# Four transformer-like layers on one core: loads in order of need, an extra step in three attentions' weaves, cross attention's keys and values inside the norm

## The chip, the cores and the metric

One core of one Trainium2 chip. The metric is the device time of one execution, in microseconds (us). Durations and waits below come from one profiled execution; a profile counts from its first instruction.

## What is computed

Input x has 2048 tokens (32 sequences of 64) of 256 channels, fp32, and a context of the same size. Four layers run one after the other on x:

- Layer 0: a transformer block, y = ln1(x), self attention with 16 heads of 16 channels, cross attention to the context (16 x 16), and an MLP to 1024 channels and back, with additive and multiplicative masks:

```python
scores = einsum('bhqd,bhkd->bhqk', q, k) / sqrt(HD)
scores = scores * mask - 10000.0 * (1.0 - mask)
probs = softmax(scores)
```

- Layer 1: a recurrent block. A state of 8 x 8 for each of 32 heads runs over the 64 tokens of a sequence, `s = k v + w * s`, read out with r; a group norm, a gate, a projection, and a second half with squared relu.
- Layer 2: two cross attentions to the context with 16 heads of 128 channels and one learned key and value beside the 64, then an MLP.
- Layer 3: a cross attention with 16 heads of 16 channels under a key mask, then an MLP. Its result is the output.

## The kernel before, in words

**Groups and stages.** The tokens are cut in 4 groups g of 512 (8 sequences). A layer of a group is a Python generator that issues instructions and yields after each step. `weave(main, (light, rate), ...)` runs `main` step by step and advances each light generator by `rate` steps for every step of main; the rates stand in `FILL` and `RATES` at the file's end. The stages:

1. layer 0 of group 0 with a filler (0.6): about 20 to 221 us
2. layer 1 of group 0 with layer 0 of group 1 (1.25) and the filler (0.7): to 528
3. layer 2 of group 0 with layer 1 of group 1 and then layer 0 of group 2 (1.13): to 965
4. layer 2 of group 1 with layer 1 of group 2 and layer 0 of group 3 (1.13): to 1403
5. layer 2 of group 2 with layer 1 of group 3 and layer 3 of group 0 (0.93): to 1773
6. layer 2 of group 3 with layer 3 of groups 1 and 2 (0.46): to about 2100
7. layer 3 of group 3 with what is left of that (1.6)

The filler, `keep`, computes layer 2's first keys and values ahead. One unit of it is four matmuls (k2p_f twice, L165; v2p_f twice, L726), one ACT step (fk, L928), one DVE step (fv, L937) and two stores of 256 KB (kd, vd) to device memory. Within what the generators issue, a scheduler places instructions on each engine by readiness; each engine then works strictly in its own order.

**Names.** DVE is VectorE, ACT ScalarE, POOL GpSimd, PE TensorE, SP the engine that issues most transfers. In tile names the letter is the norm or attention: a is layer 0's self attention, b its cross attention, c its MLP; d and e are layer 1; f, o2 and h layer 2; i and j layer 3's attention and MLP. The number behind it is the group: b1 is group 1's cross attention in layer 0.

**`norm`** (L167 to 195): statistics (L174, L176), a power on POOL (L178), the normed x (xn, L180), a bias row added to x (L185), and PE transposes to channel-major (nt, L190) with scale and offset (y, L192 and L194).

**`attn16`** (L220 to 315): for each half c of the channels, queries qT (L227) and keys kb (L232, L233; two copies, masked to one of two heads each); values vp (L242), spread by ACT and DVE into block-diagonal vb (L254, L256), with a yield after each of those four. Then four steps (c, rp): `weights` makes 16 score matmuls (sp, L269) into a two-bank tile, of which there are two; the mask (DVE product and POOL sum in layer 0, L380/381 and L385/386; one DVE sum in layer 3, L668); the softmax (L200 to 209: DVE maximum, DVE subtraction, ACT exponential, DVE sum, DVE reciprocal); and the POOL product with the reciprocal (L276). `turned` transposes the weights (tp, L286) and copies them (pt, L287); `gathered` multiplies with vb (pv, L295) and adds the bias (oT, L299). Two steps of weights are made ahead:

```python
ahead = [weights(*steps[0])]
yield
ahead.append(weights(*steps[1]))
yield
```

**Layer 1's states** (L550 to 566): vj on PE, a product on DVE (L559), two scans on DVE (L565) and a product on POOL (L566), also made two ahead, then gathered with PE (op, L588).

**Layer 2's attention** `bias_attn`: two groups of four heads run at a time, in turn (`interleave`). After the second half's product with the values (pv, L817) and its scaling (o, L828) one yield stands before the output product (`add_linear`: al_o, L328, added to x at L341).

**Loads.** At the start SP issues constants, x0, two weight slots of 512 KB, x1 to x3; POOL's queue takes the context c0 to c3 (512 KB each); ACT's takes masks and the initial state. DVE prepares masks (L153 to 159, L375, L376) as soon as they are issued in program order.

Of the kernel before, what the change touches and what calls it, by code (L numbers as in the profile page):

```python
# [14 lines left out]
P = 128  # L15
# [53 lines left out]
def kernel(  # L69
# [25 lines left out]
    def bank(name):  # L95
        return psum1.tile([P, 512], F32, tag="b1", name=name)
# [40 lines left out]

    xs, cs = [], []
    for g in range(G):
        xg = xp.tile([P, TT, D], F32, name=f"x{g}")  # L140
        nc.sync.dma_start(xg, x_in[:, g])
        xs.append(xg)
        if g == 0:
            first = [slot(L0_AT), slot(L0_AT + 1)]
    for g in range(G):
        cg = xp.tile([P, NC, GT], F32, name=f"c{g}")
        nc.gpsimd.dma_start(cg, cT[:, g])
        cs.append(cg)
    ms = cp.tile([P, S], F32, name="ms")
    for h in range(2):  # L150
        nc.scalar.dma_start(ms[64 * h : 64 * h + 64, :], m_self)
    ns = cp.tile([P, S], F32, name="ns")
    V.tensor_scalar(ns, ms, 10000.0, -10000.0, ALU.mult, ALU.add)  # L153
    V.tensor_scalar_mul(ms, ms, 0.25)
# [3 lines left out]
    at3 = VAT["L3_xattn_q_b"]  # L158
    V.tensor_scalar_mul(bq3, vt[:, at3 : at3 + NC], 0.25)

# [5 lines left out]

    def norm(xg, wname, bname, nm, y, xn, then=None):  # L167

# [12 lines left out]
        if then is not None:  # L181
# [3 lines left out]
            PL.tensor_tensor(xg, xg, row.to_broadcast([P, TT, D]), ALU.add)  # L185
        yield
        for c in range(NC):
            tp = bank(f"nt_{nm}_{c}")
            for i in range(TT):
                PE.transpose(tp[:, i * P : (i + 1) * P], xn[:, i, c * P : (c + 1) * P], ident)  # L190
# [4 lines left out]
        return y  # L195

# [145 lines left out]

    def mlp(xg, y, w1, w2, b1, func, new, nm):
        hs = []
# [22 lines left out]
    def layer0(g, work):  # L367

        xg = xs[g]
        wa = first if g == 0 else [slot(L0_AT), slot(L0_AT + 1)]  # L370
        mc = sm.tile([P, 4, S], F32, tag="mc", name=f"mc{g}", bufs=1)
        for h in range(2):
            nc.scalar.dma_start(mc[64 * h : 64 * h + 64, :, :], m_cross[:, h, 4 * g : 4 * g + 4, :])
        nr = sm.tile([P, 4, S], F32, tag="nr", name=f"nr{g}", bufs=1)
        V.tensor_scalar(nr, mc, 10000.0, -10000.0, ALU.mult, ALU.add)  # L375
        V.tensor_scalar_mul(mc, mc, 0.25)  # L376

# [9 lines left out]

        def normed(i, nm, then):
            y = work.four(f"y_{nm}")
            return norm(xg, f"L0_xattn_ln{i}_s", f"L0_xattn_ln{i}_b", nm, y, work.four(f"xn_{nm}"), then)  # L390

        y = yield from normed(1, f"a{g}", "L0_xattn_b_ao")
        yield
        bn = "L0_xattn_b_qkv"
        o = yield from attn16(
            y, y, (wa[0], 0, 512), (wa[0], 256, 512), (wa[1], 0),
            cols(bn, 0), cols(bn, 2), cols(bn, 4), mask_self, work, f"a{g}",
        )
        add_linear(xg, wa[1], 512, halves(o), f"a{g}")
        yield  # L400
        wb = [slot(L0_AT + 2), slot(L0_AT + 3)]
        y = yield from normed(2, f"b{g}", "L0_xattn_b_co")
        yield
        bn = "L0_xattn_b_kv"
        o = yield from attn16(
            y, cs[g], (wb[0], 0, D), (wb[0], 512, D), (wb[1], 0),
            cols("L0_xattn_b_q"), cols(bn, 0), cols(bn, 2), mask_cross, work, f"b{g}",
        )
        add_linear(xg, wb[1], 512, halves(o), f"b{g}")
# [30 lines left out]
    def layer1(g, work):  # L440
# [213 lines left out]
    def layer3(g, work, wp=lw):  # L654
# [15 lines left out]
        y = yield from norm(  # L670
            xg, "L3_xattn_ln1_w", "L3_xattn_ln1_b", f"i{g}", work.four(f"y_i{g}"), work.four(f"xn_i{g}"),
            "L3_xattn_cproj_b",
        )
        yield
        o = yield from attn16(
            y, cs[g], (wa[0], 0, D), (wa[0], 512, D), (wa[1], 0),
            [bq3[:, c : c + 1] for c in range(NC)], cols("L3_xattn_k_b"), cols("L3_xattn_v_b"), mask_keys,
            work, f"i{g}", 0.25,
        )
        add_linear(xg, wa[1], 512, halves(o), f"i{g}")  # L680
# [7 lines left out]
        w2 = [slot(L3_AT + 4 + i, wp) for i in range(2)]  # L688
        yield from mlp(xg, y, w1, w2, "L3_xattn_fc_b", AF.Gelu_apprx_tanh, pairs(work, f"j{g}"), f"j{g}")
        nc.sync.dma_start(out[:, g], xg)  # L690

# [39 lines left out]
    def bias_attn(a, qd, g, hh, pool, w2, work):  # L731
# [128 lines left out]
        gathered(1, p1)  # L860
        yield
        add_linear(xs[g], wo, 0, outs, f"o2{nm}")
        yield
# [234 lines left out]
```

## Time and profile before

| | us |
|---|---|
| median of 3 runs | 2218.61 (2216.74 to 2219.75) |
| the profiled execution's own time | 2216.37 |
| its span, first to last instruction | 2214.6 |
| PE busy | 2057.4 (93%) |
| DVE, ACT, POOL busy | 1097.3, 632.9, 597.5 |

The profile's columns: an instruction group is named by line, engine and operation, then output<-input with tile names (buffer numbers left out), then its shape and count. PE is TensorE's matmuls, PEld its weight loads, which overlap them. A wait is named by the group that waited, an arrow, and the group whose end released it. PEclk is the TensorE clock that was granted: 1.00 is full. In the rows of 40 slices each digit is a tenth of busy share (or of full clock), one digit for 55.4 us.

### The profile page before, as it was taken

The numbers are of one execution on the slowest core, as the hardware profiler recorded it, in microseconds if no ns is written. First come the engines' busy times: TensorE is split into PE (matmuls) and PEld (weight loads), VectorE is DVE, ScalarE is ACT, GpSimd is POOL, SyncE is SP. The second block draws the span as 40 slices with busy tenths as digits, with TensorE's granted clock in tenths as the row PEclk, the third lists the DMA queues.
The fourth block names the chain that finished last, engine by engine and source line by source line (L and its number), as shares of the span: only waits on it lengthen the run. The fifth ranks groups of instructions, "written<-read, shape, count | busy, mean of one in ns | idle before, by whom it ended". The sixth has DMA issues, their size and how long they took to land. (4 is left out here: it accounts for less than half of the span.)

```text
span 2214.6 us, 36273 instructions
## 1 busy us (share of the span) xinstructions
PE 2057.4 (93%) x15264; PEld 1242.9 (56%) x15264; DVE 1097.3 (50%) x1885; ACT 632.9 (29%) x1000; POOL 597.5 (27%) x498
## 2 busy tenths in 40 slices
PE   5889998899999898999997999999999999999998
PEld 3445444354555465755554656555566767565665
DVE  3552557423655636335556463266564355424661
ACT  1222322132321322232313132322233233222442
POOL 2331344213423314214324141233221112200220
PEclk9999998999999999999998999999999999999999
DMA  7233231226412212243121123341213342213010
GB/s 247 93 106 118 93 110 57 93 101 229 141 49 64 66 41 63 92 132 109 55 62 58 42 79 96 121 134 44 86 45 108 100 152 69 78 51 94 22 41 20
DMA packets 79794, 197.25 MB, mean 89 GB/s; under 512 B 9616, under 2 KB 14352, under 8 KB 79632
## 3 DMA queue, kind: packets, MB, share of 16 engines
q1 hardware_dynamic: 77472, 191.88, 27.1%
q8 instruction: 121, 1.98, 0.4%
q0 software_dynamic: 576, 2.10, 0.3%
q10 hardware_dynamic: 1584, 0.95, 0.2%
q14 instruction: 41, 0.34, 0.1%
HBM read 158.98 MB, written 35.91 MB: 88 GB/s over the span
## 5 line engine op out<-in xcount | busy, mean ns | idle before, releaser
L165 PE MATMUL q2p<-h,w 128*128 128x512 f32 x512 | 245.4, 612 | 6.8 <-DMA w<-in_wts 3.2
L328 PE MATMUL al_o<-w,o 128*128 128x256 f32 x1024 | 235.1, 388 | 11.7 <-DVE o L828 10.7
L328 PEld LDWEIGHTS al_o<-w,o 128*128 128x128 f32 x1024 | 196.6, 194 | 52.6 <-issue 20.6
L778 ACT ACTIVATE q<-q2p,vt 128x512 f32<-128x512 f32 x128 | 87.5, 685 | 278.9 <-PE q2p L165 275.7
L165 PEld LDWEIGHTS q2p<-h,w 128*128 128x128 f32 x512 | 94.9, 193 | 123.6 <-issue 105.5
L796 POOL TENSOR_TENSOR pn<-s,sm 128x512 f32<-128x512 f32 x64 | 69.7, 1091 | 285.2 <-DVE sm L209 198.2
L165 PE MATMUL k2p_f<-c,w 128*128 128x512 f32 x256 | 131.2, 634 | 4.9 <-DMA w<-in_wts 2.8
L726 PE MATMUL v2p_f<-w,c 128*128 128x512 f32 x256 | 122.4, 601 | 0.0
L165 PE MATMUL k2p<-c,w 128*128 128x512 f32 x256 | 120.7, 597 | 0.0
L726 PE MATMUL v2p<-w,c 128*128 128x512 f32 x256 | 119.1, 609 | 1.1 <-DVE k L764 1.1
L566 POOL TENSOR_TENSOR a<-a,r 128x1024 f32<-128x1024 f32 x32 | 76.1, 2378 | 109.8 <-DVE a L565 96.4
L937 DVE TENSOR_TENSOR fv<-v2p_f,vb 128x512 f32<-128x512 f32 x64 | 43.9, 687 | 124.7 <-PE v2p_f L726 124.7
L928 ACT ACTIVATE fk<-k2p_f,vt 128x512 f32<-128x512 f32 x64 | 43.9, 686 | 175.4 <-PE k2p_f L165 146.8
L341 DVE TENSOR_TENSOR x<-al_o,x 128x512 f32<-128x512 f32 x64 | 43.6, 683 | 101.2 <-PE al_o L328 101.2
L828 DVE TENSOR_SCALAR o<-pv,vt 128x256 f32<-128x256 f32 x128 | 55.8, 473 | 76.6 <-PE pv L817 76.4
L764 DVE TENSOR_SCALAR k<-k2p,vt 128x512 f32<-128x512 f32 x64 | 47.4, 743 | 91.4 <-PE k2p L165 91.4
L788 PEld LDWEIGHTS s2p<-k,q 128*64 128x64 f32 x2048 | 67.7, 138 | 40.8 <-issue 29.7
L817 PEld LDWEIGHTS pv<-pt,v 64*64 64x64 f32 x4096 | 72.8, 140 | 26.6 <-issue 18.4
L565 DVE TENSOR_TENSOR_SCAN a<-ws,a 128x512 f32<-128x512 f32 x64 | 85.4, 1368 | 1.7
L726 PEld LDWEIGHTS v2p_f<-w,c 128*128 128x128 f32 x256 | 49.6, 195 | 63.5 <-issue 61.3
L817 PE MATMUL pv<-pt,v 64*64 64x64 f32 x4096 | 81.7, 226 | 3.2 <-issue 1.5
L165 PEld LDWEIGHTS k2p<-c,w 128*128 128x128 f32 x256 | 49.4, 193 | 62.1 <-issue 59.4
(305 smaller groups left out, 3678.5 us busy)
## 6 DMA issues: line engine op xcount, KB each, us to landing
w<-in_wts SPq DMA_DIRECT2D x200, 512.0 KB, 3.7
kd<-fk SPq DMA_DIRECT2D x64, 260.0 KB, 2.1
k<-kd SPq DMA_DIRECT2D x64, 260.0 KB, 3.8
vd<-fv SPq DMA_DIRECT2D x64, 256.0 KB, 2.0
v<-vd SPq DMA_DIRECT2D x64, 256.0 KB, 4.5
vb<-in_vrow SPq DMA_DIRECT2D x20, 256.0 KB, 4.1
vs<-in_vrow SPq DMA_DIRECT2D x20, 256.0 KB, 3.4
c<-in_cT POOLq DMA_DIRECT2D x4, 512.0 KB, 11.6
```

What stands on the lines that cost most here:

```text
L165: PE.matmul(ps, w[:, o : o + cols], y[:, kc, :], start=(kc == 0), stop=(kc == NC - 1))
L328: PE.matmul(ps[:, a, :], y[kc][:, i * P : (i + 1) * P], wk[:, o : o + D], start=(kc == 0), stop=(kc == k - 1),)
L565: V.tensor_tensor_scan(a[:, i, :], ws[:, c, :], a[:, i, :], 0.0, ALU.mult, ALU.add)
L566: PL.tensor_tensor(a, a, r[:, c : c + 1, :].to_broadcast([P, 2, GT]), ALU.mult)
L726: PE.matmul(ps, cs[g][:, kc, bp * P : (bp + 1) * P], wv[:, 512 * kc : 512 * kc + 512], start=(kc == 0), stop=(kc == NC - 1),)
L764: V.tensor_scalar_add(k[:, :, :S], bt(ps), vec(f"L2_xattn_bk{a}", hd))
L778: A.activation(q, ps, AF.Identity, bias=vec(f"L2_xattn_bq{a}", hd))
L788: PE.matmul(sp[64 * h2 : 64 * h2 + 64, b // 4, (b % 4) * (S + 1) : (b % 4 + 1) * (S + 1)], qs[h2][:, b * S : (b + 1) * S], ks[h2][:, b, :] ...
L796: PL.tensor_tensor(pn, s[:, :, :S], rc.unsqueeze(2).to_broadcast([P, GB, S]), ALU.mult)
L817: PE.matmul(pv[b2][rows, to : to + S], vals[bp][half, hc : hc + 64], pt[half, bp, h2 * S : (h2 + 1) * S], start=True, stop=True,)
L828: V.tensor_scalar_add(ov[:, :, 1, :], src[1], bv)
L928: A.activation(k[:, :, :S], bt(ps), AF.Identity, bias=vec("L2_xattn_bk1", hd))
```

## The change

1. **Loads.** x0 is the first load on SP, ahead of the constants. The self mask and c0 go by ACT's queue (c0 was on POOL's); c1 to c3 stay on POOL's. x1 to x3 are issued in `layer0(g)`, not at the start. The preparation of the self mask and of layer 3's query bias moves behind the first norm (`prepare`), that of a group's cross mask behind its self attention.
2. **`attn16` is cut in three**: `queries16` (both halves, one yield), `keys16` (keys of both halves and the values, a yield each), and `attn16` (scores to output). In the cross attentions (layer 0's b, layer 3's i) `keys16` runs inside `norm`, between the normed x and its transposes; it used to stand behind them.
3. **Extra yields**: in `attn16` behind the second weights made ahead; in layer 1 behind the second states; in layer 2 between the last product with the values and the output product.
4. **Output**: layer 3's result is stored in two halves of 256 KB, each behind its addition, not in one of 512 KB.
5. **Rates**: `FILL` (0.6, 0.7) to (0.58, 0.68); the first four `RATES` (1.25, 1.13, 1.13, 0.93) to (1.2, 1.08, 1.08, 0.88).

The number of matmuls and of transposes is the same.

```diff
+    xs = [xp.tile([P, TT, D], F32, name=f"x{g}") for g in range(G)]
+    cs = [xp.tile([P, NC, GT], F32, name=f"c{g}") for g in range(G)]
+    nc.sync.dma_start(xs[0], x_in[:, 0])
+    ms = cp.tile([P, S], F32, name="ms")
+    for h in range(2):
+        nc.scalar.dma_start(ms[64 * h : 64 * h + 64, :], m_self)
+    nc.scalar.dma_start(cs[0], cT[:, 0])
     ct = cp.tile([P, C_N], F32, name="ct")
...
-    for g in range(G):
-        xg = xp.tile([P, TT, D], F32, name=f"x{g}")
-        nc.sync.dma_start(xg, x_in[:, g])
...
+    first = [slot(L0_AT), slot(L0_AT + 1)]
+    for g in range(1, G):
+        nc.gpsimd.dma_start(cs[g], cT[:, g])
...
+    def prepare():
+
+        at3 = VAT["L3_xattn_q_b"]
+        tc.keep_in_program_order(V.tensor_scalar(ns, ms, 10000.0, -10000.0, ALU.mult, ALU.add))
+        V.tensor_scalar_mul(ms, ms, 0.25)
+        V.tensor_scalar_mul(bq3, vt[:, at3 : at3 + NC], 0.25)
...
-    def norm(xg, wname, bname, nm, y, xn, then=None):
+    def norm(xg, wname, bname, nm, y, xn, then=None, between=None):
...
         yield
+        got = (yield from between) if between is not None else None
         for c in range(NC):
             tp = bank(f"nt_{nm}_{c}")
...
-    def attn16(yq, ykv, wq, wk, wv, bq, bk, bv, masked, work, nm, scale=1.0):
+    def queries16(yq, wq, bq, work, nm, scale=1.0):
 
         qT = work.four(f"qT_{nm}")
-        kb = []
         for c in range(NC):
             qp = bank(f"qp_{nm}_{c}")
             linear(qp, wq[0], wq[1] + c * P, wq[2], yq)
             A.activation(qT[:, c, :], qp, AF.Identity, bias=bq[c], scale=scale)
+        yield
+        return qT
+
+    def keys16(ykv, wk, wv, bk, work, nm):
+
+        kb = []
+        for c in range(NC):
             kp = bank(f"kp_{nm}_{c}")
...
+        return kb
+
+    def attn16(qT, kb, bv, masked, work, nm):
+
         oT = work.four(f"oT_{nm}")
...
         ahead.append(weights(*steps[1]))
         yield
+        yield
...
         for two, ps in token_linear(w2, 0, hs, nm):
             V.tensor_tensor(xg[:, two, :], ps, xg[:, two, :], ALU.add)
+            if to is not None:
+                nc.sync.dma_start(to[:, two, :], xg[:, two, :])
             yield
...
     def layer0(g, work):
 
         xg = xs[g]
+        if g:
+            nc.sync.dma_start(xg, x_in[:, g])
...
+        y = yield from normed(1, f"a{g}", "L0_xattn_b_ao")
+        if g == 0:
+            prepare()
+        yield
+        bn = "L0_xattn_b_qkv"
+        qT = yield from queries16(y, (wa[0], 0, 512), cols(bn, 0), work, f"a{g}")
+        kb = yield from keys16(y, (wa[0], 256, 512), (wa[1], 0), cols(bn, 2), work, f"a{g}")
+        o = yield from attn16(qT, kb, cols(bn, 4), mask_self, work, f"a{g}")
+        add_linear(xg, wa[1], 512, halves(o), f"a{g}")
+        yield
...
+        wb = [slot(L0_AT + 2), slot(L0_AT + 3)]
+        bn = "L0_xattn_b_kv"
+        y, kb = yield from normed(
+            2, f"b{g}", "L0_xattn_b_co", keys16(cs[g], (wb[0], 512, D), (wb[1], 0), cols(bn, 0), work, f"b{g}")
         )
...
         ahead.append(states(*todo[1]))
         yield
+        yield
...
         gathered(1, p1)
+        yield
         yield
         add_linear(xs[g], wo, 0, outs, f"o2{nm}")
...
-FILL, KV_BUFS = (0.6, 0.7), 6
-RATES = (1.25, 1.13, 1.13, 0.93, 0.46, 1.6)
+FILL, KV_BUFS = (0.58, 0.68), 6
+RATES = (1.2, 1.08, 1.08, 0.88, 0.46, 1.6)
```

More of the change, by code (lines that the diff above doesn't have):

```diff
@@ L136, in cols @@
         return [vec(name, at), vec(name, at + 1)]
-    xs, cs = [], []
-    for g in range(G):
-        xg = xp.tile([P, TT, D], F32, name=f"x{g}")
-        nc.sync.dma_start(xg, x_in[:, g])
[L142 to L151, printed above, removed]
+    first = [slot(L0_AT), slot(L0_AT + 1)]
+    for g in range(1, G):
+        nc.gpsimd.dma_start(cs[g], cT[:, g])
     ns = cp.tile([P, S], F32, name="ns")
-    V.tensor_scalar(ns, ms, 10000.0, -10000.0, ALU.mult, ALU.add)
-    V.tensor_scalar_mul(ms, ms, 0.25)
     s0t = cp.tile([P, NC, 8, B], F32, name="s0t")
@@ L157 @@
     bq3 = cp.tile([P, NC], F32, name="bq3")
-    at3 = VAT["L3_xattn_q_b"]
-    V.tensor_scalar_mul(bq3, vt[:, at3 : at3 + NC], 0.25)
+    def prepare():
[3 more added lines that the diff above has]
+        V.tensor_scalar_mul(bq3, vt[:, at3 : at3 + NC], 0.25)
     def linear(ps, w, at, step, y, cols=P):
@@ L194, in norm @@
                 A.activation(y[:, c, :], tp, AF.Identity, bias=vec(bname, c), scale=vec(wname, c))
-        return y
+        return y if between is None else (y, got)
     def softmax(s, src, n, nm, scale=1.0):
@@ L341, in add_linear, with mlp @@
             V.tensor_tensor(xg[:, two, :], ps, xg[:, two, :], ALU.add)
-    def mlp(xg, y, w1, w2, b1, func, new, nm):
+    def mlp(xg, y, w1, w2, b1, func, new, nm, to=None):
         hs = []
@@ L369, in layer0 @@
         xg = xs[g]
+        if g:
+            nc.sync.dma_start(xg, x_in[:, g])
         wa = first if g == 0 else [slot(L0_AT), slot(L0_AT + 1)]
[L371 to L376, printed above, removed]
         def mask_self(s, sp):
@@ L386, in mask_cross, with normed @@
             PL.tensor_tensor(sv, sv, over_heads(nr), ALU.add)
-        def normed(i, nm, then):
+        def normed(i, nm, then, between=None):
             y = work.four(f"y_{nm}")
-            return norm(xg, f"L0_xattn_ln{i}_s", f"L0_xattn_ln{i}_b", nm, y, work.four(f"xn_{nm}"), then)
+            return norm(
+                xg, f"L0_xattn_ln{i}_s", f"L0_xattn_ln{i}_b", nm, y, work.four(f"xn_{nm}"), then, between
+            )
         y = yield from normed(1, f"a{g}", "L0_xattn_b_ao")
+        if g == 0:
+            prepare()
         yield
         bn = "L0_xattn_b_qkv"
[L395 to L398, printed above, removed]
+        qT = yield from queries16(y, (wa[0], 0, 512), cols(bn, 0), work, f"a{g}")
+        kb = yield from keys16(y, (wa[0], 256, 512), (wa[1], 0), cols(bn, 2), work, f"a{g}")
+        o = yield from attn16(qT, kb, cols(bn, 4), mask_self, work, f"a{g}")
         add_linear(xg, wa[1], 512, halves(o), f"a{g}")
         yield
+        mc = sm.tile([P, 4, S], F32, tag="mc", name=f"mc{g}", bufs=1)
+        for h in range(2):
+            nc.scalar.dma_start(mc[64 * h : 64 * h + 64, :, :], m_cross[:, h, 4 * g : 4 * g + 4, :])
+        nr = sm.tile([P, 4, S], F32, tag="nr", name=f"nr{g}", bufs=1)
+        tc.keep_in_program_order(V.tensor_scalar(nr, mc, 10000.0, -10000.0, ALU.mult, ALU.add))
+        V.tensor_scalar_mul(mc, mc, 0.25)
         wb = [slot(L0_AT + 2), slot(L0_AT + 3)]
-        y = yield from normed(2, f"b{g}", "L0_xattn_b_co")
+        bn = "L0_xattn_b_kv"
+        y, kb = yield from normed(
+            2, f"b{g}", "L0_xattn_b_co", keys16(cs[g], (wb[0], 512, D), (wb[1], 0), cols(bn, 0), work, f"b{g}")
+        )
         yield
[L404 to L408, printed above, removed]
+        qT = yield from queries16(y, (wb[0], 0, D), cols("L0_xattn_b_q"), work, f"b{g}")
+        o = yield from attn16(qT, kb, cols(bn, 2), mask_cross, work, f"b{g}")
         add_linear(xg, wb[1], 512, halves(o), f"b{g}")
@@ L668, in mask_keys @@
             V.tensor_tensor(sv, pv, over_heads(mk), ALU.add)
-        y = yield from norm(
+        y, kb = yield from norm(
             xg, "L3_xattn_ln1_w", "L3_xattn_ln1_b", f"i{g}", work.four(f"y_i{g}"), work.four(f"xn_i{g}"),
-            "L3_xattn_cproj_b",
+            "L3_xattn_cproj_b", keys16(cs[g], (wa[0], 512, D), (wa[1], 0), cols("L3_xattn_k_b"), work, f"i{g}"),
         )
         yield
[L675 to L679, printed above, removed]
+        qT = yield from queries16(y, (wa[0], 0, D), [bq3[:, c : c + 1] for c in range(NC)], work, f"i{g}", 0.25)
+        o = yield from attn16(qT, kb, cols("L3_xattn_v_b"), mask_keys, work, f"i{g}")
         add_linear(xg, wa[1], 512, halves(o), f"i{g}")
@@ L688, in layer3 @@
         w2 = [slot(L3_AT + 4 + i, wp) for i in range(2)]
-        yield from mlp(xg, y, w1, w2, "L3_xattn_fc_b", AF.Gelu_apprx_tanh, pairs(work, f"j{g}"), f"j{g}")
-        nc.sync.dma_start(out[:, g], xg)
+        yield from mlp(xg, y, w1, w2, "L3_xattn_fc_b", AF.Gelu_apprx_tanh, pairs(work, f"j{g}"), f"j{g}", out[:, g])
     def interleave(parts, lag, most=2):
```

## The prediction

> **What bounds the kernel now.** I read the page first (its parts 1 and 2), then what TensorE waited for, then windows and timelines around the longest waits.
>
> ```profile
> span 2214.6 us, 36273 instructions
> PE 2057.4 (93%) x15264; PEld 1242.9 (56%) x15264; DVE 1097.3 (50%) x1885; ACT 632.9 (29%) x1000; POOL 597.5 (27%) x498
> PE   5889998899999898999997999999999999999998
> PEclk9999998999999999999998999999999999999999
> ```
>
> TensorE is the bound: 93% of the span, no other engine over 50%. The change adds and removes no matmul, so PE's work at full clock stays. What can move is the rest: idle time (2214.6 - 2057.4 = 157 us) and the time lost at a lowered clock (clock 0.970 over the run; in the granted-clock records 133.7 us stand at 0.5, always in multiples of 3.41 us, and nearly every one begins in or just behind a wait of PE). So I add up waits, site by site, before and after. TensorE's waits:
>
> ```profile
> PE tp_a L286 <- POOL s_a L276: 20.4, 6, 5.9
> PE nt_a L190 <- DVE xn_a L180: 19.8, 1, 19.8
> PE tp_b L286 <- POOL s_b L276: 13.9, 6, 7.1
> PE al_o L328 <- DVE o L828: 10.7, 5, 3.2
> PE sp_a L269 <- DVE s L205: 10.4, 4, 4.7
> PE op L588 <- POOL a L566: 5.9, 4, 2.1
> ```
>
> Columns: microseconds in all, times, longest. The transposes in front of P·V (tp) wait for a softmax; the start waits for the first norm; layer 2's output product (al_o) waits for its last scaled rows (o). Windows over three such places:
>
> ```profile
> 0.00:20.00 20.00, 0.24 (x1) 0.18 (x1) 3.62 (x19) 1.28 (x1) 7.37 (x14) 1.00 0.91 300
> 349.00:404.00 55.00, 40.76 (x226) 19.31 (x218) 41.99 (x40) 13.12 (x18) 30.51 (x19) 0.78 0.12 46
> 600.00:612.00 12.00, 7.91 (x24) 4.93 (x23) 11.07 (x12) 0.00 (x0) 7.34 (x5) 0.72 0.24 86
> 640.00:646.00 6.00, 4.48 (x73) 3.15 (x74) 1.95 (x4) 1.54 (x4) 1.60 (x2) 0.72 0.01 3
> ```
>
> After the window's length come the busy times of PE, PE's weight loads, DVE, ACT, POOL, then clock, DMA share, GB/s. In the first 20 us the DMA engines are 91% busy at 300 GB/s, PE hardly at all. 349 to 404 is group 1's cross attention: PE 74% busy at clock 0.78, the kernel's worst stretch.
>
> **The price of the clock.** Between 604.98 and 611.81 the record stands at 0.5, 2.2 us of it idle: 4.6 us of PE work at half speed, 2.3 us lost. So a wait that goes takes about one stretch with it, 1.7 to 2.3 us. A wait of 2.11 us (at 641.5) was enough to bring 3.41 us at 0.5, which the fourth window shows. The Trainium skill ("TensorE: Matmul & The Clock Gate", HAM oscillation) speaks of idle gaps over some 3.4 us; by that rule the short waits would cost no clock, and the forecast below would gain about 5 us less in layer 2. The row decides.
>
> **1. Loads.** x1 to x3 (3 x 0.52 MB = 1.57 MB) leave their place ahead of the filler's first weight. That weight landed at 24.65 and released PE at 24.79. 1.57 MB at 0.300 MB/us is 5.2 us: **5.2 gained**. The first norm begins earlier too (its statistics stood on DVE until 16.25, behind the masks' two steps at 15.71), but then PE waits for the weights, so this adds nothing. Bounds: 0, if the first weights' issue on SP is held behind the context that now goes by ACT's queue (the state tensor there, issued at 2.0, landed at 12.8), to 9 us. x1 to x3 come behind, some 200 us before their use; the masks of the cross attention are still loaded long before.
>
> **2. The 16-channel attentions.** The chain of one softmax (a0, group 0's self attention) now:
>
> ```profile
> 47.23 1.10 PE L269 MATMUL sp_a<-kb_a,qT_a 32*64 32x128 f32 x32
> 48.40 1.22 DVE L380 TENSOR_TENSOR s_a<-sp_a,ms 128x1024 f32<-128x1024 f32 x1 [0.37 <-PE sp_a L269]
> 49.71 2.35 POOL L381 TENSOR_TENSOR s_a<-s_a,ns 128x1024 f32<-128x1024 f32 x1 [13.45 <-DVE s_a L380]
> 58.64 1.22 DVE L200 TENSOR_REDUCE mx_a<-s_a 128x16 f32<-128x1024 f32 x1 [1.25 <-POOL s_a L381]
> 59.77 0.24 DVE L209 RECIPROCAL sm_a<-sm_a 128x16 f32<-128x16 f32 x1
> 60.16 2.72 POOL L276 TENSOR_TENSOR s_a<-s_a,sm_a 128x1024 f32<-128x1024 f32 x1 [1.56 <-DVE sm_a L209]
> 62.93 1.97 PE L286 MATMUL tp_a<-ct,s_a 128*128 128x128 f32 x8 [5.79 <-POOL s_a L276]
> ```
>
> From the end of the scores (48.33) to the transposes: 14.6 us. The operations alone are 4 x 1.22 + 0.24 on DVE, 2.35 + 2.72 on POOL, 1.06 on ACT: 11.25; the rest is DVE working in order: the second softmax's maximum (58.64) stands ahead of the first's reciprocal. PE work between scores and transposes, the cover, was 8.9 us, hence 5.79 idle. An extra step in the weave adds cover only where something stands in it, so I counted the cover in the instruction order of both kernels, with rows' durations (a 128x512 matmul 0.86, a filler unit of four 3.44, a group of 16 score matmuls 1.04, a transpose 0.11).
>
> Stage with the filler, group 0: the first two score groups now stand together and a filler unit behind them. Cover of the first transposes 8.9 -> 9.5: the wait stays. The third softmax is scored later and stands behind two others on DVE and POOL: ready some 32 us from the start against 25.6 of PE work: **5.6 lost** in a0, the same pattern **2.7 lost** in b0. The last norm of the layer (nt_d0) now comes directly after its last product, cover 3.4 -> 0 against the norm's chain of 4.0: **4.8 lost** with its clock; 0.5 gained at nt_c0. Sum **-12.6**.
>
> Group 1, beside layer 1's recurrence: in b1 five filler units (17.2 us) stood between first scores and last product, now six, with the recurrence's pairs spread among them, PE work 35.0 -> 39.3 us; the cover of the first transposes rises from 10.6 to 15.4. The six waits there (1.40, 0.60, 2.97, 3.73, 5.47, 1.48: 15.65 us) shrink to 6.5 by the covers, and of 24 us at 0.5 (18.5 of them busy: 9.3 lost) one stretch stays: 9 + 8 = **17 gained**, and **3** in a1 (waits 4.0 -> 1). Sum **+20**; from 5 to 25, which is all that stands there.
>
> Groups 2 and 3, beside layer 2: self attention 11.6 of waits; the first two (4.46, 0.62) go since the cover doubles (10.1 -> 21.4), but the transposes of the third softmax lose cover (19.4 -> 13.9): as much again. **0**, from -6 to +6 each.
>
> **3. Layer 2's output product.** Around 600 us DVE runs four scans and two products of the recurrence between the o's, so op waits 0.84 and al_o 0.90 and 3.18. With the added step, the o's stand ahead of that state in DVE's order and another 6.9 us of work on PE: 4.9 + 2.4 of clock, **7.4 gained** in each of two stages, **4.4** in the fourth (2.66 at 1826 and its stretch).
>
> **4. Keys and values in the norm.** nt_b's cover goes from 2.8 to 21.9 us: 1.3 gained in each of groups 2 and 3, and about 1.0 in the cross attention behind. But everything that follows moves nearer to its producer. The norm of the MLP (nt_c) has 1.1 instead of 7.2 us against a chain of 5.4, its first product 0 instead of 1.1 against 1.0: **-6.5** with clock; nt_e 2.8 -> 1.7 (**-1.1**), kk 10.3 -> 4.5 against 6.3 (**-1.5**), the first queries 3.4 -> 0 (**-1**). Together with 3: 7.4 + 1.3 + 1.0 - 6.5 - 1.1 - 1.5 - 1.0 = **-0.4** a stage, -0.8 for two. Third layer-2 stage: dwp 2.0 -> 1.1 and nt_e3 11.2 -> 4.3: **-2**.
>
> **5. The tail.** The last output transfer is half as long: 512 KB took from 2210.8 to the end at 2214.6, 3.8 us; 256 KB stores (vd) take 2.0: **1.8 gained**. The last attention (i3) loses the MLP products that stood between its last scores and transposes: 9.7 -> 2.8 us against a chain of 10.2, **-7.5** with clock; nt_i3 +0.95, nt_j2 -0.4. Sum **-5**.
>
> **Sum**: 5.2 - 12.6 + 20 - 0.8 - 2 + 4.4 - 5.1 = 9.1 us gained. The profiled execution took 2216.37 us (span 2214.6), so 2207.3 by its own time; the median of the runs (2218.61) stands 2.2 above it: **2209 us**.
>
> **Another rule that speaks against it.** At 386.92 four scans on DVE took 7.75 us (1.94 each) beside POOL's products; the median of all 64 is 1.21. The Trainium skill ("SBUF — State Buffer", Who interferes with whom) says that a DVE instruction with two inputs in SBUF and a GpSimd one that reads SBUF exclude each other. By it two softmaxes moved together would cost each other more; by the rows above (L205 at 1.18 to 1.22) not in a0. My sum has nothing for it.
>
> **The rivals.**
> *The slack works as named* (0.14): the waits for softmaxes and states (tp_a 20.4, tp_b 13.9, sp_a 10.4, op 5.9) vanish by half, 25 us, with six stretches of 1.7, 10 us; with 7.0 from the start and the end, less 5 for part 4, that is 37, 2182: a case from 2175 to 2199. For it: those are the longest rows. Against: the covers counted above.
> *The waits only move* (0.17): b1 gains 10 instead of 20, and the sum is near nothing: 2214 to 2223. For it: the total of matmuls is the same and most sites here trade one wait for another.
> *The chain becomes the bound: slower* (0.33). Where two score groups follow each other without work between, the second softmax's rows get into DVE's and POOL's queues ahead of the first's reciprocal; that costs 57.4 to 59.8, 2.4 us, in a0 today. If it costs 2.4 more in each of 12 attentions, 9.1 - 28.8 gives 2238; with half of that, 2224. It decides from 0.8 us an attention (9.1 / 12) to nothing gained, from 1.1 to a slower kernel. For it: a0, b0 and i3 already show it in the order of instructions. Against: in the layer-2 stages something always stands between.
>
> **Chances.** Under 0.2% (4.4 us) a measurement of this kernel can't tell a difference from no change. Forecast 0.36 (2199 to 2214), larger gain 0.14, nothing 0.17, slower 0.33 (2223 to 2238): faster 0.50, same 0.17, slower 0.33. The range leaves out the ends of the outer cases: 2187 to 2232; the forecast's own is 2199 to 2214.
>
> **What would show it.** First filler product near 19.5 instead of 24.8; waits of tp_a in group 0 up by some 5, a new wait at nt_d0; in 349 to 404 PE over 85% busy and clock over 0.9; no al_o wait for o; new waits at nt_c in groups 2 and 3 and at tp_i at the end; an end within 2.5 us of the last addition. I am wrong above all if the chains' lengths, which I took from this trace, change with the new order on DVE and POOL, or if b1 keeps its clock loss.

## The result, and the profile after

The changed kernel takes 2230.15 us (median of 4 executions, 2225.29 to 2233.71); the kernel before 2218.12 (4 executions, 2216.74 to 2219.75). The ratio is 1.0052, 95% interval 1.0032 to 1.0073: **slower by half a per cent**, where 2209 was forecast. The profiled execution took 2230.37 us, 14.0 more than the one of before.

The first lines of the changed kernel's page, with the PE and clock rows of the 40 slices:

```profile
span 2228.6 us, 36274 instructions
...
PE 2073.6 (93%) x15264; PEld 1252.8 (56%) x15264; DVE 1095.5 (49%) x1885; ACT 633.4 (28%) x1000; POOL 594.2 (27%) x497
...
PE   6889989999989898999898989999999999999997
...
PEclk9999999999999898999998989999999999999998
```

PE is busy 16.2 us longer for the same matmuls, so the loss isn't idle time. Idle time up to the last matmul is 150.9 us, before 152.7. The rest is the clock. I split each trace in three: idle time of PE; half of PE's busy time in the stretches that the clock record puts at 0.5; and what is left, the work at full clock. (The record begins at 28.1 and 25.6 us. Ahead of it the filler's 128x512 matmuls start 0.85 us apart and behind it 0.43, so that stretch counts as 0.5 too.) Work is 2000.2 us before and 2000.7 after: the split closes. **Idle -1.8 us, clock 57.2 -> 72.9, +15.7 us.** Over all 18 traces of this study work lies between 1996.6 and 2002.6 us. Each split is of one execution, and those of the kernel before spread from 2211.4 to 2223.1 us, so a few us in a stage's clock share need not be the change's doing.

TensorE's longest waits after the change (microseconds in all, times, longest):

```profile
PE tp_a L296 <- POOL s_a L286: 14.3, 4, 5.1
PE nt_a L190 <- DVE xn_a L179: 12.6, 1, 12.6
PE s2p L803 <- DVE s L205: 10.3, 4, 2.8
PE tp_b L296 <- POOL s_b L286: 7.9, 2, 5.1
PE nt_c L190 <- DVE xn_c L179: 7.3, 3, 3.5
PE k2p_f L164 <- DMA w<-in_wts: 6.4, 1, 6.4
...
PE pv L832 <- DVE oT_b L309: 5.1, 2, 2.6
PE tp_i L296 <- POOL s_i L286: 4.8, 1, 4.8
...
PE nt_d L190 <- DVE xn_d L179: 3.6, 1, 3.6
...
PE al_o L339 <- DVE o L843: 2.7, 3, 1.2
```

The waits that the change aimed at did shrink: tp_a 20.4 -> 14.3, tp_b 13.9 -> 7.9, al_o 10.7 -> 2.7, sp_a <- s 10.4 -> gone. In their place stand s2p (layer 2's scores, for layer 2's softmax subtraction s on DVE), nt_c, nt_d, pv (for oT_b) and tp_i, none of which took more than 1.3 us before. The sizes changed too: behind the start, PE's idle gaps above 4 us went from 7 to 3, those above 2 us from 20 to 28. The clock record has 38 windows of 3.41 us at 0.5 before and 46 after (the last one, behind the work, left out). All of them lie on one grid of 3.41 us that runs through the trace. Of the windows at full clock, 13 held 2.0 us or more of PE's idle time before and 22 after; each of these was followed by one at 0.5.

The loss (idle + clock, us) by stage, cut at PE's first transposes of the next norm in each trace; "expected" is what my terms gave:

| stage | before | after | gained | expected |
|---|---|---|---|---|
| 1, with the start (to nt_d of group 0) | 40.0 + 7.7 | 38.3 + 12.7 | -3.4 | -7.4 |
| 2, layer 1 of group 0 (to nt_f) | 20.5 + 11.0 | 13.7 + 10.0 | +7.7 | +20 |
| 3, layer 2 of group 0 | 35.4 + 15.2 | 35.0 + 17.3 | -1.7 | -0.4 |
| 4, layer 2 of group 1 | 32.3 + 15.1 | 32.2 + 15.5 | -0.2 | -0.4 |
| 5, layer 2 of group 2 | 7.1 + 1.7 | 7.7 + 0.0 | +1.1 | -2 |
| 6, layer 2 of group 3 (to its nt_h) | 9.2 + 1.7 | 10.6 + 3.4 | -3.1 | +4.4 |
| 7, the end | 8.1 + 4.8 | 13.4 + 13.9 | -14.4 | -5.1 |

The end as windows from the last layer 2's MLP norm on (length, then PE busy, weight loads, DVE, ACT, POOL, clock, DMA share, GB/s), before and after:

```profile
2067.00:2214.60 147.60, 134.61 (x916) 89.10 (x916) 70.33 (x114) 57.90 (x77) 29.54 (x17) 0.96 0.09 31
```

```profile
2071.00:2228.60 157.60, 140.20 (x886) 92.34 (x885) 64.11 (x108) 55.16 (x74) 27.65 (x16) 0.89 0.09 29
```

10 us longer, 4.4 of them idle, at 0.89 of the clock instead of 0.96. The changed kernel's timeline of PE, DVE and POOL there shows the new wait:

```profile
2169.08 1.10 PE L279 MATMUL sp_i<-kb_i,qT_i 32*64 32x128 f32 x32
2170.25 1.22 DVE L687 TENSOR_TENSOR s_i<-sp_i,mk 128x1024 f32<-128x1024 f32 x1 [1.08 <-PE sp_i L279]
...
2176.43 0.25 DVE L209 RECIPROCAL sm_i<-sm_i 128x16 f32<-128x16 f32 x1
2176.83 1.90 POOL L286 TENSOR_TENSOR s_i<-s_i,sm_i 128x1024 f32<-128x1024 f32 x1 [5.62 <-DVE sm_i L209]
2178.79 1.97 PE L296 MATMUL tp_i<-ct,s_i 128*128 128x128 f32 x8 [4.78 <-POOL s_i L286]
```

The last scores are made at 2169, when the neighbour's MLP is used up. PE has 3.8 us of transposes and products left, to 2174.0; then nothing until the softmax is through.

### The profile page after: what moved, and what is told of

It reads as the page before. It is cut to its first block, busy times and chain, and to the rows that moved or that the text cites. A ratio compares the mean times of both kernels' runs of the same rounds, so it can differ in the third digit from the quotient of the medians.

```text
span 2228.6 us, 36274 instructions
## 1 busy us (share of the span) xinstructions
PE 2073.6 (93%) x15264; PEld 1252.8 (56%) x15264; DVE 1095.5 (49%) x1885; ACT 633.4 (28%) x1000; POOL 594.2 (27%) x497
## 5 line engine op out<-in xcount | busy, mean ns | idle before, releaser
L339 PE MATMUL al_o<-w,o 128*128 128x256 f32 x1024 | 230.2, 383 | 3.7 <-DVE o L843 2.7
L803 PEld LDWEIGHTS s2p<-k,q 128*64 128x64 f32 x2048 | 69.7, 140 | 55.2 <-issue 45.1
L803 PE MATMUL s2p<-k,q 128*64 128x65 f32 x2048 | 79.5, 227 | 14.6 <-DVE s L205 10.3
```

Source lines behind the costliest of these rows:

```text
L339: PE.matmul(ps[:, a, :], y[kc][:, i * P : (i + 1) * P], wk[:, o : o + D], start=(kc == 0), stop=(kc == k - 1),)
L803: PE.matmul(sp[64 * h2 : 64 * h2 + 64, b // 4, (b % 4) * (S + 1) : (b % 4 + 1) * (S + 1)], qs[h2][:, b * S : (b + 1) * S], ks[h2][:, b, :] ...
```

## The experiments

Every kernel was timed beside the kernel before on its chip; before's medians there were 2217.7 to 2218.2. Ratios are to it. Generators' steps are counted from the code: layer 0 has 46 steps before and 50 after, layer 3 29 and 31, layer 2 90 and 98, layer 1 45 and 46.

### Parts taken back, and the loads alone

**l3_as_before**: the changed kernel with layer 3's attention as before the change, so without the extra step there.

```diff
-        y, kb = yield from norm(
+        y = yield from norm(
...
-            "L3_xattn_cproj_b", keys16(cs[g], (wa[0], 512, D), (wa[1], 0), cols("L3_xattn_k_b"), work, f"i{g}"),
+            "L3_xattn_cproj_b",
...
-        qT = yield from queries16(y, (wa[0], 0, D), [bq3[:, c : c + 1] for c in range(NC)], work, f"i{g}", 0.25)
+        qT = work.four(f"qT_i{g}")
+        query = query_half(qT, y, (wa[0], 0, D), [bq3[:, c : c + 1] for c in range(NC)], f"i{g}", 0.25)
+        kb = yield from keys16(cs[g], (wa[0], 512, D), (wa[1], 0), cols("L3_xattn_k_b"), work, f"i{g}", query)
```

> The changed kernel with layer 3's attention as it was: keys and values behind the norm, beside the queries, and no extra step behind the second scores there; all else changed. Theory T (the loss sits in the last 330 us, in layer 3's attentions: their keys went into the norm, so the MLP products of the neighbour group are used up before the last softmax needs them; and there the clock stays at 0.5 longer): some 11 to 14 us come back, 2215 to 2219, and the wait of tp_i of 4.8 us is gone. Rival S (the score groups of layer 0 now stand together, the softmax chain on DVE and POOL bounds): little comes back, 2226 to 2232.

Measured 2242.81, ratio 1.0112 (1.0097 to 1.0127). Both theories miss: it became slower still. Stage 5 lost 27.1 instead of 7.7, and the end still 26.2, so theory T is not shown by this. With two steps fewer at unchanged rates, layer 3 ran ahead of layer 2; rates_late_as_changed takes that up.

**no_score_step**: without the extra step in `attn16`.

```diff
         ahead.append(weights(*steps[1]))
         yield
-        yield
```

> The changed kernel without the extra step behind the second score group in all twelve 16-channel attentions. T: most of the loss stays, since keys and values are still in layer 3's norm: 2224 to 2234. S: the loss goes, 2214 to 2220, with group 0's waits of tp_a and tp_b smaller.

Measured 2215.30, ratio 0.9987 (0.9978 to 0.9996): the figure of S, but not by its mechanism. The first stage changed by 1.7 only; stages 3 and 4 lose 42.3 and 37.7 instead of 52.3 and 47.7. The waits of group 0 stay (tp_a 9.0 at 64.6). So the 10 us a stage lie beside layer 2. Stages 2 and 5 lose 5.3 and 4.2 us more than the changed kernel's.

**rates_before**: the changed kernel with the old rates.

```diff
-FILL, KV_BUFS = (0.58, 0.68), 6
-RATES = (1.2, 1.08, 1.08, 0.88, 0.46, 1.6)
+FILL, KV_BUFS = (0.6, 0.7), 6
+RATES = (1.25, 1.13, 1.13, 0.93, 0.46, 1.6)
```

> The changed kernel with the six rates and two fill rates as before. T: the rates of the last two stages were not changed, so the tail stays as it is: 2225 to 2234, with groups 0 to 3's norms in other places. Rival R (the lower rates leave more light work for the end of each stage): 2215 to 2222.

Measured 2258.84, ratio 1.0185 (1.0171 to 1.0199), beyond both. Stage 5 lost 34.4 and stage 2 35.7: with the old rates the light work ends early (at layer 2's step 86 of 98 in stages 3 and 4 and 84 in stage 5, for 90 and 89) and the norm of layer 2's MLP stands without cover (nt_h 15.5 us in 4 waits). Stage 2's longest waits are tp_b's, 6.76 and 3.94 us.

**before_loads_out**: the kernel before with parts 1 and 4 (loads, output in halves) alone.

> The kernel before with the loads' part and the output in halves alone. From the changed kernel's trace: the first filler product starts at 21.2 instead of 24.8 (3.6 us) and the time from the last matmul to the end falls from 4.5 to 4.0: 2214, if the waits behind it are those of before (2211 to 2217). My prediction's figure was 7.0 for the two: 2211. Any rival in which the loads collide with something later: 2218 or more.

Measured 2208.52, ratio 0.9959 (0.9946 to 0.9971): 9.2 gained at the median. In its trace the first filler product starts 3.9 us earlier (20.9) and stages 1 and 2 lose 7.1 less; from stage 3 on it loses about as much as before (132.6 for 130.7). This part of the change is good by itself: 9.2 at the median, 6.6 between the profiled executions.

### Place or number of steps, and three parts alone

**step_moved**: the extra step behind the last product of `attn16`, not behind the second scores.

```diff
         ahead.append(weights(*steps[1]))
         yield
-        yield
...
                 pts = []
                 yield
+        yield
         return oT
```

> The changed kernel with the extra step of the 16-channel attention put behind its last product instead of behind the second scores: as many steps of each generator and the same rates as the changed kernel. Theory P (it is the place of the step that costs: it shifts what follows in the attention against layer 2's steps, so that the MLP's norm of groups 2 and 3 lands without cover): as without the step, 2212 to 2220, no wait of nt_c over 2 us. Rival C (it is the count: one more step a light attention delays the light work against the rates): as the changed kernel, 2226 to 2234.

Measured 2234.30, ratio 1.0062 (1.0046 to 1.0078): stages 3 and 4 at 52.5 and 51.2, like the changed kernel, with the same wait of nt_c of 3.54. Theory P falls in this form: wherever the step stands in the attention, what follows it comes later.

**combo1**: no extra step in the attentions, layer 3 as before, the rates of stages 5 and 6 scaled to the steps.

```diff
-RATES = (1.2, 1.08, 1.08, 0.88, 0.46, 1.6)
+RATES = (1.2, 1.08, 1.08, 0.845, 0.42, 1.6)
```

> The changed kernel without the extra step in the attentions, with layer 3's attention as before, and with the rates of the third layer-2 stage and the fourth (0.845 and 0.42) such that the light generators stand at the same share of layer 2's steps as before the change. Sum from the runs: without the step the first four stages lose 158.5 us to idle time and clock (before 177.3), and the stages behind, as before the change, 32.6 to 37.5: 2192 to 2198. Rival (the earlier run with layer 3 as before was slower for what layer 3 does, not for its rates): 2205 or more.

Measured **2196.09**, ratio 0.9897 (0.9884 to 0.9910), as the sum had it. So layer 3's old order was not what made l3_as_before slow.

**product_step_alone**: the kernel before with the step ahead of layer 2's output product, rates (1.25, 1.04, 1.04, 0.855, 0.422, 1.6). The edit is against the kernel before.

```diff
         gathered(1, p1)
         yield
+        yield
         add_linear(xs[g], wo, 0, outs, f"o2{nm}")
```

> The kernel before with the extra step ahead of layer 2's output product alone, rates scaled by 90/98 for layer 2's eight further steps. My prediction's terms: 7.4 in each of two stages and 4.4 in the fourth: 19 gained, 2199. Rival (the o's stand ahead in DVE's order but other waits take over): 2212 to 2222.

Measured 2214.69 over 12 executions (2210.40 to 2220.44), ratio 0.9982 (0.9971 to 0.9993): 3.5 gained where 19 was forecast, in the rival's range. Its idle time fell by 4.8 and 5.0 us in stages 3 and 4: my term was 4.9. The clock's part of the term didn't come: stage 3 lost 14.6 us to it (before 15.2), stage 4 19.9 (before 15.1), and the end 11.2 for 4.8. The profiled execution was the slowest of the twelve, so how much of that is its own spread stays open.

**keys_alone**: the kernel before with layer 0's keys in the norm and queries in a step of their own, fill 0.575, rates (1.3, 1.155, 1.155, 0.93, 0.46, 1.6).

> The kernel before with layer 0's keys and values of the cross attention inside the norm alone (queries in a step of their own), rates scaled to layer 0's 48 steps instead of 46. Prediction's terms without the steps: nt_b's wait gone, 1.3 a group, nothing else sized: 2213 to 2218. Rival (what followed the norm moves nearer to its producer): 2220 to 2232.

Measured 2223.36, ratio 1.0026 (1.0015 to 1.0037). Stage 1 loses 55.7 for 47.7; stages 2 to 4 gain 2.3, 1.0 and 2.4. That is in the rival's range. In group 0, where only the filler runs beside, tp_a waits 8.98 us (5.79 before) and nt_d 3.63 (0.2 before); whether the moved keys do this or the queries' own step isn't told apart.

### Layer 3's keys, the step with scaled rates, two combinations

**combo_l3_keys**: combo1 with layer 3's keys and values inside its norm again, rates (1.2, 1.08, 1.08, 0.855, 0.44, 1.6).

> Combo1 (2196: no extra step in the attentions, layer 3 as before, rates in the same share) with layer 3's keys and values inside its norm, rates scaled to the one step more. My prediction's term for the tail is -7.5 for tp_i, whose cover falls from 9.7 to 2.8: 2203 (2200 to 2206), the wait of tp_i near 4.8 us back. Rival (the tail's loss in the changed kernel is chance of the clock alone): 2193 to 2199.

Measured 2204.74, ratio 0.9939 (0.9926 to 0.9952): 8.65 slower than combo1; the forecast's term was 7.5. But the end itself loses only 2.1 more than combo1's (25.2 for 23.1: idle 3.1 more, clock 1.0 less), and stages 3 and 5 lose 3.2 and 3.6 more. So this brings the wait back, and doesn't show that the 8.65 are the end's. The wait of 4.78 us:

```profile
PE tp_i L296 <- POOL s_i L286: 4.8, 1, 4.8
```

**combo_score_step**: combo1 with the extra step in layer 0's attentions, fill 0.56, rates (1.25, 1.103, 1.103, 0.845, 0.42, 1.6).

> Combo1 with the extra step behind the second scores in layer 0's eight attentions, fill and rates scaled so that every stage keeps its share of steps. Theory C (the step cost 15 us in the changed kernel because the light work ran late against rates that did not follow): 2190 to 2199. Theory P (in the layer-2 stages the extra step itself moves the MLP's norm behind its producer): 10 lost in each of two stages, 5 gained beside layer 1: 2208 to 2214, with nt_c waits of 3.5.

Measured 2218.05, ratio 0.9998 (0.9989 to 1.0007): 22 slower than combo1. Theory C falls too: keeping the shares didn't help, though the light work ends at layer 2's step 88 in both. Stages 3 and 4 lost 52.8 and 48.3, but by other waits than the changed kernel: al_d 8.15 (3.17 there) and kk 2.65 beside nt_c 2.17.

**combo2**: combo1 with group 0's attentions of layer 0 in the old order, fill 0.6 (the cross attention's part of the edit).

```diff
...
+        if g == 0:
+            y = yield from normed(2, f"b{g}", "L0_xattn_b_co")
+            yield
+            qT = work.four(f"qT_b{g}")
+            kb = yield from keys16(*ofk, query_half(qT, y, wq, cols("L0_xattn_b_q"), f"b{g}"))
+        else:
+            y, kb = yield from normed(2, f"b{g}", "L0_xattn_b_co", keys16(*ofk))
+            yield
+            qT = yield from queries16(y, wq, cols("L0_xattn_b_q"), work, f"b{g}")
...
```

> Combo1 with group 0's attentions of layer 0 in the order of before (keys and values behind the norm, beside the queries), fill 0.6. The first stage lost 48.8 us to idle time and clock in combo1, 55.7 with the keys in the norm alone, 43.7 with loads and output alone: 5 gained, 2189 to 2193. Rival (group 0 is bound by the softmax chain either way): 2194 to 2199.

Measured 2191.56, ratio 0.9879 (0.9866 to 0.9893); 4.5 gained for 5, and stage 1 at 44.4.

**combo3**: combo2 with the extra step in group 1's attentions, rate 1.25.

> Combo2 with the extra step behind the second scores in group 1's two attentions alone, beside layer 1, rate 1.25 there. With the step that stage lost 23.8 us, without it 29.1: 5 gained over combo2, 2184 to 2190. Rival (the 5 us are the clock's chance): equal to combo2 within 3.

Measured 2195.88, ratio 0.9895 (0.9880 to 0.9910): 4.3 slower than combo2, a miss of the other sign. Stage 2 lost 30.6 where combo2 lost 24.8, so the changed kernel's 23.8 there isn't the step's doing alone.

### Rates alone

All four are combo2 with one or two rates changed; no generator is touched.

**rate_106**: 1.06 for 1.08 beside layer 2 of groups 0 and 1. The edit against combo2:

```diff
-RATES = (1.2, 1.08, 1.08, 0.845, 0.42, 1.6)
+RATES = (1.2, 1.06, 1.06, 0.845, 0.42, 1.6)
```

> Combo2 (2191.6) with the rate beside layer 2 of groups 0 and 1 at 1.06 for 1.08: the light work ends at layer 2's step 90 of 98 and not 88. Theory L (what costs is where the light steps stand beside layer 2's, whatever moved them): each of these two stages, now 45 and 38 us of loss, moves by 5 to 10 us, up most likely: 2200 to 2212. Theory S (the step itself costs): 2189 to 2195.

Measured 2213.76, ratio 0.9981 (0.9969 to 0.9993): 22 slower than combo2, a little beyond theory L's range. Stages 3 and 4 lose 54.7 and 46.8 (combo2's 45.1 and 38.2). Its waits, first, and combo2's:

```profile
PE pv_b L315 <- DVE k L802: 10.4, 2, 5.7
PE nt_c L190 <- DVE xn_c L179: 8.2, 3, 3.5
```

```profile
PE v2p L764 <- DVE k L802: 9.1, 2, 4.6
...
PE nt_c L190 <- DVE xn_c L179: 1.1, 1, 1.1
```

That is the changed kernel's wait of nt_c (3.54 at 883.5; there 3.54 at 885.0), without its step: in both the light work ends at layer 2's step 90 of 98, in combo2 at 88. So that wait, and 18 us of loss in the two stages, need no extra step: it is enough that the light steps stand later beside layer 2's, two at the end. The wait isn't all of it: al_d waits 5.49 us for 3.17 in both stages as well.

**rate_110**: 1.10 for 1.08.

> Combo2 with that rate at 1.10: the light work ends at step 87. Theory L: the loss of the two stages moves by 5 to 10 us each, with the wait of al_d (8.2 us in combo_score_step, whose rate was 1.103) there: 2205 to 2213. Theory S: 2189 to 2195.

Measured 2193.45, ratio 0.9896 (0.9881 to 0.9911): 2 slower than combo2, in theory S's range. In the trace al_d waits 8.15 us as in combo_score_step (so that wait is the rate's, not the step's), but no wait of nt_c stands behind it; the two stages lose 6.4 more than combo2's, and the end 3.9 less by the clock. So theory L has its size in one run only. And the step isn't cleared: combo_score_step and rate_110 run at the same pace (1.103 and 1.10) and share the 8.15, yet the former loses 11.4 more in these stages. It ends its light work at step 88, rate_110 at 87; whether the step or that one place costs this, the runs don't tell apart.

**rates_late_as_changed**: the changed kernel's 0.88 and 0.46 for 0.845 and 0.42.

> Combo2 with the rates of the third and fourth layer-2 stage as in the changed kernel, 0.88 and 0.46, for 0.845 and 0.42: the light work of the third ends at step 87 and not 90, and in the fourth 4 more steps of layer 3 are used up, so 13 and not 17 are left for the end. Theory (layer 3's old order was slow for its rates): the third stage loses some 20 more as in that run (27 for 4.7) and the end some 3: 2210 to 2218. Rival: within 5 of combo2.

Measured 2217.83, ratio 1.0001 (0.9993 to 1.0010): 26 slower than combo2. Stage 5 lost 27.3 for 4.7, the end 26.5 for 23.2. That is l3_as_before's stage 5 (27.1), and its longest wait is that of layer 2's MLP with nothing beside it:

```profile
PE tp_i L306 <- POOL s_i L296: 8.4, 2, 4.8
PE h_h L164 <- DVE hm L192: 8.2, 2, 6.8
```

The tp_i wait of 4.8 is here too, with layer 3's old order: with 13 instead of 17 steps of the neighbour left, the last softmax is as bare as with the keys in the norm. So in these runs layer 3's old order is slow under the changed kernel's rates and not under combo2's.

**more_left**: 0.40 for 0.42, so 19 steps are left for the end.

> Combo2 with 0.40 for 0.42 in the fourth stage: 19 steps of layer 3 are left beside the last group's instead of 17. If the end (23.2 us of loss, before the change 12.9) lacks work of the neighbour beside its softmaxes, 3 to 6 gained: 2186 to 2189. If not, within 3 of 2191.6, or slower by the fourth stage's waits.

Measured **2190.06** (2189.74 to 2190.62), ratio 0.9873 (0.9861 to 0.9886), the fastest kernel of this study. The end loses 15.8 for 23.2, but 7.0 of these 7.4 are clock (6.3 for 13.3), and stage 6 gives back 3.9: the count of waits there hardly changed. I don't claim the 1.5 us between this and combo2 for the neighbour's work.

## Why the prediction was wrong

**What bounds it, and that the work is the same.** Right: 2000.2 and 2000.7 us of work.

**The price of the clock.** This is the step that failed most. "A wait that goes takes about one stretch with it, 1.7 to 2.3 us": I added it to waits that go and to some that come, from one example. In the whole trace idle time fell by 1.8 us while the clock cost 15.7 more. The change cut long waits into several middling ones (above 4 us: 7 -> 3; above 2 us: 20 -> 28), and a long wait starts no more stretches than a middling one. In a0, the wait of 5.79 us before (to 62.9) started one stretch at 0.5, of 6.83 us; those of 5.08 and 2.45 us after (to 63.4 and 79.6) started two, of 6.83 and 3.41. So the windows that hold 2.0 us or more of idle time went from 13 to 22, and stretches at 0.5 from 25 to 29. I read this from the traces; no run changed the number of waits at equal idle time.

**1. Loads: 5.2 gained.** Direction right, size 3.6 (24.79 -> 21.22): the second weights left SP at 12.17 and the filler's first at 15.74, not earlier. With what follows it gave 9.2 in the run with loads and output alone, more than the start shows. Idle time there fell by 7.3 us in stages 1 and 2, the start's 3.9 among them.

**2. Group 0, -12.6.** a0 and nt_d were right as sites, too large in size: a0 waits 5.08 + 2.45 for 5.79 before, 1.7 more where 5.6 was forecast, and nt_d 3.63, its chain put at 4.0. b0 was wrong: tp_b waits 5.08 + 2.86 for 9.5 before, less and not 2.7 more. The idle time of the stage fell by 1.7, the loads' 3.6 among it; 5.0 more went to the clock.

**2. Group 1, +20.** b1 was right: 16.5 gained for 17. a1 was wrong: 7.1 lost for 3 gained. I took its waits (4.0) to shrink; instead, scores waited 2.80 for a mixing product of layer 1 on DVE (sp_a <- xm) and layer 1's product 2.73 for POOL's (vp <- xm), with three windows at 0.5. The stretch measured, from one norm's transposes to the next's, now holds b1's keys too. The wait for xm doesn't hang on the extra step: it is 3.27 in no_score_step and 2.54 with the loads alone (0.85 before). I had counted the cover in front of a1's transposes, but not who stands ahead in DVE's and POOL's order for the mixing.

**3 and 4. Stages 3 and 4, -0.4 each.** Measured -1.7 and -0.2, but only in part by the named waits: al_o's and nt_b's are gone (the former's idle -4.8 and -5.0 were measured alone), nt_c's is there with 3.54 + 0.69, nt_e's 0.9 longer; kk's didn't come. The extra step in the attentions of groups 2 and 3, which part 2 put at 0 (from -6 to +6 each), was the costliest: without it the two stages lose 10.0 less each (no_score_step), though their light work then ends two steps earlier as well. The largest change had no term: sp_a's wait for layer 2's softmax subtraction s on DVE (10.4) went, and s2p waits 10.3 for the same s in its place. And the cause of nt_c's wait was not the one given. Keys and values stand in the norm in combo2 as well, without that wait; rate_106 brings it back with a rate. So part 4's -6.5 belongs to steps and rates together: the light work, with two steps more a group for the scores, ends at 90 instead of 88 at the same rate.

**3. The fourth layer-2 stage, +4.4.** Measured -3.1: al_o's wait for o shrank by 0.7 only (2.66 to 1.24 and 0.70), another al_o waits 1.06 for ACT's pt at 2045.7, pv_i 1.92 where pv waited 1.51, and one more window stands at 0.5 (1.7 us). Idle time is 1.4 more. Stage 5: +1.1 for -2.

**5. The end, -5.1.** The wait was right: tp_i waits 4.78 (forecast 7.5 with its clock), idle is 5.3 more, and combo_l3_keys brings the wait back. The size was not: 9.1 more went to the clock. That isn't the keys' doing alone: combo1 and combo2, with layer 3's old order and no such wait, lose 13.3 to the clock there too. The shorter store gave 0.5 (last matmul to end 4.57 -> 4.04), not 1.8: the last 256 KB took 3.3 us (2225.3 to 2228.6), not 2.0.

**Where the sign turned.** The terms miss by 12.3 in stage 2, 9.3 at the end, 7.5 in stage 6 and 1.1 in stages 3 and 4; they were too dark by 4.0 in stage 1 and 3.1 in stage 5: 9.1 forecast, 23.1 short, 14.0 lost.

**The rivals.** The slower case got the sign and its range (2223 to 2238) holds 2230, but by luck: its mechanism, a softmax chain made longer by DVE's order, isn't there in group 0 (from a0's first mask product to its transposes 14.6 us for 14.5), and taking the step away left group 0's stage within 1.7 us. I gave it 0.33. What none of the rivals named is the rate: a step added to a woven generator moves all that comes behind it, and so does the rate.

## What to carry to other kernels

Where generators are woven at fixed rates, an extra step is not local: count, for each stage, at which step of the main work the light work ends, and time the neighbouring rates before the edit is judged (here 88 of 98 against 90 was worth some 9 us a stage, and in stage 5 step 87 instead of 90 cost 22). Keeping the old place is no safe rule: the kernel before ended at 82 of 90, eight steps from the end, as the changed one does at 90 of 98, and combo_score_step, at 88 with the extra step, lost as much as rate_106 at 90 without it (101.1 and 101.5 us in the two stages). Judge an edit by idle time and clock time apart, stage by stage, with the work at full clock as a check that the split closes. Parts that are good alone (loads in order of need, 9 us) can be hidden by others in the same change: taking it back part by part and setting the rates anew turned +12 us into -28.

## What the runs showed of the hardware

A wait's price in clock depends on more than its length. In the changed kernel's trace two waits of 2.45 us (at 79.6 and 2070.8) are followed by one window of 3.41 us at 0.5 and by three:

```profile
78.00:85.00 7.00, 5.38 (x15) 3.12 (x16) 2.10 (x4) 2.30 (x4) 3.88 (x5) 0.76 0.10 37
2068.00:2082.00 14.00, 11.55 (x72) 5.95 (x57) 10.21 (x17) 5.05 (x5) 4.19 (x3) 0.63 0.18 47
```

In combo2 the three windows behind such a wait (2.10 us, 2033.2 to 2043.5) hold no idle time of PE at all:

```profile
2033.00:2047.00 14.00, 13.92 (x87) 8.08 (x88) 12.41 (x15) 6.57 (x7) 4.26 (x2) 0.63 0.16 47
```

So being busy is not enough to get the clock back in the next window. What PE runs there differs: the first two windows hold score matmuls, whose weights are 32x64, and transposes; the third is filled by the MLP's matmuls of 128x512 (from PE's rows in that stretch):

```profile
2033.57 1.14 PE L289 MATMUL sp_i<-kb_i,qT_i 32*64 32x128 f32 x18
...
2036.73 1.11 PE L190 MATMUL nt_h<-ct,xn_h 128*128 128x128 f32 x4
2037.77 1.98 PE L289 MATMUL sp_i<-kb_i,qT_i 32*64 32x128 f32 x30
2039.68 10.72 PE L164 MATMUL h_h<-hm,w 128*128 128x512 f32 x20
```

All 18 traces together hold 452 windows at 0.5 without idle time, and 71 of them were followed by another. None of the 71 was more than two thirds covered by 128x512 matmuls; all 197 that were ended the stretch. Of the 255 others 184 ended it too, so this is no full rule.

The fall is plainer. Of the windows at full clock in the 18 traces, all 322 with 2.0 us or more of PE's idle time were followed by one at 0.5, 94 of 240 with 1.2 to 2.0 us, and 5 of 10211 with less. The Trainium skill ("TensorE: Matmul & The Clock Gate", What's actually happening) has the clock fall after an idle window of some 3.4 us and come back after a busy one. The window's length agrees with the records (all multiples of 3.41). But waits of 1.22 us (at 403.7) and 2.45 us were enough here, the count puts the sure fall at 2.0 us of a window and not at a whole one, and one busy window did not always bring the clock back.

So the price of a wait hangs on where it lies on the grid. combo2 and rate_110 run the same instructions in the same order from stage 5 on and idle 9.9 us each at the end, but lose 13.3 and 9.3 there to the clock. In combo2 a wait of h_h (1.93 us) lies in one window and is followed by one at 0.5; in rate_110 the same wait (1.99 us) is cut by a border of the grid, 1.58 us in one window, and is followed by none. This may be why executions of one kernel differ, which no run shows: the twelve of product_step_alone spread over 10 us, the four of more_left over 0.9.
